# Layer norm of a two-layer vision block: the squares of three channel chunks added on GpSimd before TensorE sums them

## The chip, the cores and the metric

The kernel runs on one core of a Trainium2 chip. A core has five engines with a queue of instructions each: TensorE (PE in the profile; its weight loads are shown apart as PEld), VectorE (DVE), ScalarE (ACT), GpSimd (POOL) and SyncE (SP), which here issues most of the DMAs. The engines work on SBUF, a memory of 128 partitions; TensorE writes its results into PSUM. The metric is the device time of one execution in microseconds, as the median of several runs.

## The reference

The input x has the shape (8, 384, 64, 64), f32: eight images, 384 channels. Two layers follow each other, each with a group norm in front and a residual around it. The first is a window attention with a layer norm over the channels, the second a convolution block. Cut to what matters:

```python
def _L0_conv_ref(x, norm_g, norm_b, qkv_w, qkv_b, proj_w, proj_b, rpb1, rpb2):
    xt = x.reshape(b, c, h * w).transpose(0, 2, 1)
    mu = xt.mean(-1, keepdims=True)
    var = ((xt - mu) ** 2).mean(-1, keepdims=True)
    xt = (xt - mu) / jnp.sqrt(var + EPS) * norm_g + norm_b
    qkv = (xt @ qkv_w + qkv_b).reshape(b, h * w, 3, c).transpose(2, 0, 1, 3)
    ...
    x1 = win_attn(w1[0], w1[1], w1[2], rpb1, None)
    x2 = win_attn(w2[0], w2[1], w2[2], rpb2, ATTN_MASK2)
    ...
    out = out @ proj_w + proj_b

x = x + _L0_conv_ref(_gn(x), ...)
x = x + _L1_conv_ref(_gn(x), fft_filter, w_in, w_dw, w_out)
```

The change is in `mu` and `var`, the mean and the variance over the 384 channels of each of the 4096 pixels of an image.

## The kernel before

An image is cut into eight strips of 8 rows, 512 pixels each. A strip is a tile of 128 partitions by 3 chunks by 512 pixels (`strip`), so a pixel's 384 channels lie in 128 partitions and 3 chunks. There are 64 strips in all.

The first layer takes a strip through these pieces: `group_normal` (VectorE) writes the group-normed strip y. `ln_square` (L306) lets ScalarE write the squares of y, one instruction for all three chunks, into sq, a tile with a single buffer. `ln_sums` (L310) lets TensorE multiply y and sq with a column of 1/384, so that the sum over the partitions comes out; the three chunks are added up in PSUM, 4 groups of 128 pixels side by side in 32 columns of the array each. One matmul of the program appears as two in the trace (f32), so y and sq have 24 matmul instructions each per strip. From the sums come the variance, a square root and a reciprocal (tile lr, VectorE and ScalarE); a DMA writes the row to DRAM and another spreads it over the partitions (line, rs), and `ln_scale` (L333) multiplies y by it. `shifted_half` (L338) lets GpSimd copy halves of two strips into the strip y2 of the shifted windows (L349 to L351). Then come the attention's matmuls: pq (`qk_tile`), pvv (`v_tile`, with a memset of a column of v on GpSimd, L392), pS (`scores`), the soft maximum on VectorE and ScalarE (tile e, L429 to L439), pT (`turn`), pA (`apply`), the division by the sum (tile o, L473 and L474), po (`put`) and pr (`project`).

The second layer has pt (`mix`), pf (`transform`), pz (`back`), the border tiles z that ScalarE writes (L598 to L602), the convolution on VectorE (`conv`, L642, tile zz, one instruction per tap), the gate, pw (`finish`), and x_finish (L672), in which VectorE adds pw onto the strip and so frees the PSUM buffer. The tag gemm has four PSUM buffers; pw takes three of them at once.

All pieces are put into one plan by hand (`at(place, piece, ...)`), sorted by place and then written out, so that strips of the first layer of one image lie between strips of the second layer of the image before. TensorE's matmuls keep this order exactly (`keep_in_program_order`). The instructions of the other engines are ordered at build time by a list scheduler, which takes what is ready by its own estimate and otherwise follows the place in the program; each engine then works through its queue in order. For a strip, with v = u - 4 and u = 2s + 16b, the layer norm has these places:

```python
at(v + 0.15, group_normal, b, s)
at(v + 0.45, ln_square, b, s)
at(v + 0.99, ln_sums, b, s)
at(v + 1.35, ln_scale, b, s)
```

At the start GpSimd issues 64 small DMAs for the position bias (rpb_raw, L154), then memsets of the borders of seven z tiles (L268, L269), and copies six blocks of the packed q and k weights (`pack_qk`, L118). TensorE at the same time begins with the mean of the first image (pm, pv), the sums of strip 0, and the matmuls that prepare the weights (pb, pc, pv).

Of the kernel before, what the change touches and what calls it, by code (L numbers as in the profile page):

```python
# [9 lines left out]
ALU = mybir.AluOpType  # L10
AX = mybir.AxisListType

P = 128
KC = 3
# [18 lines left out]
def block_kernel(ctx: ExitStack, tc: tile.TileContext, out, x, consts, fsel, wqk, wv, bqk, bv,  # L33
                 wp, bp, lng, lnb, rpb1, rpb2, w_in, w_dw, w_out, filt):
    nc = tc.nc
# [8 lines left out]
    def psum(name):  # L44
        return ps.tile([P, ST], F32, tag="gemm", name=name)
# [6 lines left out]
    def matmul(*args, **kw):  # L52
        tc.keep_in_program_order(nc.tensor.matmul(*args, **kw))  # L53
# [4 lines left out]
    def strip(tag, bufs, name):  # L58
        return sb.tile([P, KC, ST], F32, tag=tag, bufs=bufs, name=name)

    def row512(tag, bufs, name):
        return sb.tile([P, ST], F32, tag=tag, bufs=bufs, name=name)
# [9 lines left out]
    for s in range(NS):  # L72
        tag, bufs = ("x", 5) if s < 5 else (("xn", 1), ("ow", 1), ("y2", 1))[s - 5]
        t = strip(tag, bufs, f"x_first{s}")
# [188 lines left out]
    xs, ys, y2s, qks, vs, os_, ots, x1s, zs = ({} for _ in range(9))  # L263
# [42 lines left out]
    def ln_square(b, s):  # L306
        sq = ys[b, s, "sq"] = strip("sq", 1, f"sq_{b}_{s}")
        nc.scalar.activation(sq, ys[b, s], AF.Square)

    def ln_sums(b, s):  # L310


        p = psum(f"ln_{b}_{s}")
        for to, t in ((0, ys[b, s]), (P, ys.pop((b, s, "sq")))):
            for k in range(KC):
                for j in range(4):
                    matmul(p[32 * j:32 * (j + 1), to:to + P], ones_c[:, 0:32], t[:, k, j * P:(j + 1) * P],
                           start=(k == 0), stop=(k == KC - 1))
        m = sb.tile([P, 2 * P], F32, tag="lc", bufs=1, name=f"m_{b}_{s}")
        nc.scalar.copy(m, p[:, 0:2 * P])  # L320
        rc = sb.tile([P, P], F32, tag="lr", bufs=2, name=f"lr_{b}_{s}")
        nc.vector.tensor_tensor(rc, m[:, 0:P], m[:, 0:P], ALU.mult)  # L322
        nc.vector.tensor_tensor(rc, m[:, P:2 * P], rc, ALU.subtract)
        nc.scalar.activation(rc, rc, AF.Sqrt, bias=eps_t)
        nc.vector.reciprocal(rc, rc)

        line = dr.tile([4, P], F32, tag="line", bufs=4, name=f"line_{b}_{s}")
        queue = nc.scalar if b == 0 and s < 2 else nc.sync
        queue.dma_start(out=line, in_=rc[0:P:32, :])
        rs = ys[b, s, "rs"] = row512("rs", 2, f"rs_{b}_{s}")  # L330
        queue.dma_start(out=rs, in_=bass.AP(line.tensor, line.offset, [[0, P], [1, ST]]))
# [347 lines left out]
    for b in range(B):  # L679
# [17 lines left out]
        for s in range(NS):  # L697
# [3 lines left out]
            at(v - 0.84, load, b, s, "norm")  # L701
# [5 lines that stand above are left out]
# [162 lines left out]
```

## Time and profile before

The profile is of one execution. Its device time was 3803.7 us, of which the span from the first to the last instruction is 3801.9 us.

| what | us |
|---|---|
| median of 3 runs | 3809.83 |
| lowest and highest run | 3804.54 and 3810.86 |
| device time of the profiled execution | 3803.7 |
| span of the profiled execution | 3801.9 |
| mean granted TensorE clock | 0.994 |
| TensorE, 24 matmuls ln<-y per strip, busy in all 64 strips | 56.3 |
| TensorE, 24 matmuls ln<-sq per strip, busy in all 64 strips | 54.3 |
| ScalarE, one square of a strip (64 of them) | 1.484 median |
| GpSimd, copy 128x384 f32, L349 (112 into y2) | 0.504 shortest, 0.506 median, 1.437 longest |
| VectorE, one tap of the convolution, L642 (1490) | 0.654 shortest, 0.747 median, 0.993 longest |
| TensorE waiting in pt for VectorE's x_finish | 14.5 in all, 11 times, longest 2.5 |

How to read it: busy is the time in which at least one instruction of the kind runs; matmuls overlap, so 24 of 0.27 us each can be busy for 0.85 us only. In a timeline a line gives the start and the length in us, the engine, the line of the kernel, the operation, the tile written and the tiles read, the shape, and how many instructions were merged; in square brackets stands how long the engine had been idle before and what ended that.

### The profile page before, as it was taken

Reading aid. Unit: us, or ns where it says so; the run is one execution under the profiler, and the core shown is the slowest. Engines: PE = TensorE matmul, PEld = TensorE weight load, DVE = VectorE, ACT = ScalarE, POOL = GpSimd, SP = SyncE. Lnnn points to the kernel's source line nnn. Section 1 sums busy time; section 2 is a strip of 40 time slices with the busy share of each in tenths; the row PEclk is TensorE's granted clock in tenths of the full one; section 3 lists DMA queues with packets and bytes.
Section 4 is the critical chain, followed back from the end, with each engine's and each line's share of the span. In section 5 each row is a group of like instructions: output and inputs, shape, how many; then the busy total and the mean of one; then the engine's idle time right before and its main releaser. Section 6 shows DMA issues by size and latency. Waiting matters only on the chain.

```text
span 3801.9 us, 90288 instructions
## 1 busy us (share of the span) xinstructions
PE 3681.0 (97%) x39168; PEld 2350.2 (62%) x39168; DVE 2822.1 (74%) x4601; ACT 2458.7 (65%) x3997; POOL 273.0 (7%) x648
## 2 busy tenths in 40 slices
PE   6999999999999999999999999999999999999998
PEld 4666666666666665666666666666666666666554
DVE  5555577768777678777878777778778777677898
ACT  3766577657667576666767666666676667676442
POOL 4000000000000000000000000000000000000000
PEclk9999999999999999999999999999999999999999
DMA  4322222223322223223322323323233222221422
GB/s 120 99 86 83 89 92 102 90 95 115 115 92 93 109 88 121 97 82 112 115 104 103 107 80 107 123 79 107 91 119 107 98 95 73 97 80 71 159 100 75
DMA packets 144496, 377.16 MB, mean 99 GB/s; under 512 B 12308, under 2 KB 12900, under 8 KB 144100
## 3 DMA queue, kind: packets, MB, share of 16 engines
q1 hardware_dynamic: 139952, 370.60, 27.5%
q8 instruction: 308, 5.05, 0.6%
q0 software_dynamic: 2048, 0.15, 0.1%
q10 hardware_dynamic: 2100, 0.63, 0.1%
q14 instruction: 88, 0.72, 0.1%
HBM read 270.54 MB, written 100.79 MB: 98 GB/s over the span
## 4 chain that ended last, share of the span: by engine, by line
PE 82%; DVE 10%; DMA 3%; ACT 2%; issue 2%; SPq 0%; DVEq 0%; ACTq 0%
PE pq L53 22%; PE pt L53 13%; PE pr L53 12%; PE pvv L53 11%; PE pw L53 6%; DVE zz L642 4%; PE pS L53 3%; PE pz L53 3%; PE pT L56 3%; PE pA L53 2%; PE ln L53 2%; PE po L56 2%; PE pf L53 2%; DMA rs<-line 1%; PE pc L53 1%
## 5 line engine op out<-in xcount | busy, mean ns | idle before, releaser
L642 DVE SCALAR_TENSOR_TENSOR zz<-z,dw_sb,zz 128x512 f32<-128x512 f32 x1490 | 1094.8, 751 | 132.5 <-ACT z L601 114.6
L53 PE MATMUL pq<-y,wqk_sb 128*128 128x512 f32 x2160 | 990.6, 596 | 0.4 <-issue 0.4
L53 PEld LDWEIGHTS pq<-y,wqk_sb 128*128 128x128 f32 x2160 | 403.1, 190 | 457.4 <-issue 426.2
L53 PE MATMUL pt<-wi_sb,xn 128*128 128x384 f32 x1536 | 540.7, 490 | 14.5 <-DVE x_finish L672 14.5
L53 PE MATMUL pr<-oT,wp_sb 128*128 128x512 f32 x1152 | 523.5, 593 | 1.1 <-DVE oT L507 1.0
L53 PE MATMUL pvv<-wv_sb,y 128*128 128x192 f32 x2880 | 495.8, 326 | 0.0
L53 PEld LDWEIGHTS pvv<-wv_sb,y 128*128 128x128 f32 x2880 | 471.7, 190 | 36.2 <-issue 21.8
L53 PEld LDWEIGHTS pt<-wi_sb,xn 128*128 128x128 f32 x1536 | 287.9, 191 | 223.8 <-issue 60.0
L367 ACT ACTIVATE qab<-pq,bq_sb,cst 96x512 f32<-96x512 f32 (+1 forms) x256 | 197.2, 770 | 303.0 <-PE pq L53 301.3
L367 ACT ACTIVATE kcd<-pq,vec 32x512 f32<-32x512 f32 x512 | 348.8, 681 | 8.9
L53 PEld LDWEIGHTS pr<-oT,wp_sb 128*128 128x128 f32 x1152 | 210.9, 190 | 225.1 <-issue 210.9
L322 DVE TENSOR_TENSOR lr<-m 128x128 f32<-128x128 f32 x64 | 18.8, 294 | 437.3 <-ACT m L320 437.3
L553 ACT COPY t<-pt 128x384 f32<-128x384 f32 x256 | 122.8, 480 | 194.4 <-PE pt L53 191.8
L401 ACT COPY v<-pvv 128x384 f32<-128x384 f32 x256 | 121.6, 479 | 177.2 <-PE pvv L53 176.9
L367 ACT ACTIVATE qcd<-pq,bq_sb,cst 96x512 f32<-96x512 f32 (+1 forms) x256 | 197.9, 773 | 56.3 <-PE pq L53 49.2
L516 DVE SCALAR_TENSOR_TENSOR x_add<-pr,vec,x_add 128x512 f32<-128x512 f32 x192 | 143.5, 748 | 120.2 <-PE pr L53 118.4
L349 POOL COPY y<-y 128x384 f32<-128x384 f32 x112 | 99.8, 891 | 1741.9 <-PE pvv L53 1243.6
L636 ACT ACTIVATE zz<-z,dw_sb 128x512 f32<-128x512 f32 x183 | 133.2, 732 | 89.0 <-PE pw L53 56.0
L367 ACT ACTIVATE kab<-pq,vec 96x512 f32<-96x512 f32 (+1 forms) x256 | 174.8, 683 | 21.5 <-PE pq L53 19.4
L439 ACT ACTIVATE e<-e 128x1024 f32<-128x1024 f32 x128 | 135.4, 1058 | 74.9 <-DVE e L434 73.8
L53 PE MATMUL pw<-zz,wo_sb 128*128 128x512 f32 x384 | 182.9, 612 | 0.0
L56 PEld LDWEIGHTS po<-cst,o 128*128 128x128 f32 x1024 | 119.7, 141 | 64.2 <-issue 62.8
(139 smaller groups left out, 5286.9 us busy)
## 6 DMA issues: line engine op xcount, KB each, us to landing
x_add<-in_x_dram SPq DMA_DIRECT2D x64, 768.0 KB, 9.6
x1d<-x_add SPq DMA_DIRECT2D x64, 768.0 KB, 3.6
x_mix<-x1d SPq DMA_DIRECT2D x64, 768.0 KB, 4.3
x_finish<-x1d SPq DMA_DIRECT2D x64, 768.0 KB, 4.4
out_dram<-x_finish SPq DMA_DIRECT2D x64, 768.0 KB, 4.5
x_norm<-in_x_dram SPq DMA_DIRECT2D x61, 768.0 KB, 7.4
x_stats<-in_x_dram SPq DMA_DIRECT2D x56, 768.0 KB, 7.5
rs<-line SPq DMA_DIRECT2D x62, 256.0 KB, 3.0
```

The costliest lines, as they stand in the source:

```text
L53: tc.keep_in_program_order(nc.tensor.matmul(*args, **kw))
L56: tc.keep_in_program_order(nc.tensor.transpose(*args, **kw))
L322: nc.vector.tensor_tensor(rc, m[:, 0:P], m[:, 0:P], ALU.mult)
L349: nc.gpsimd.tensor_copy(dst[:, :, :, :, 0:4], src[:, :, :, :, 4:8])
L367: return nc.scalar.activation(dst[to:to + n], pq[of:of + n], AF.Identity, bias=bias[of:of + n], scale=scale)
L401: nc.scalar.copy(v[:, 2 * g:2 * g + 2, :, 0:HD], pvv[:, 0:384].rearrange("p (g h d) -> p g h d", g=2, h=4))
L439: nc.scalar.activation(e, e, AF.Exp)
L516: nc.vector.scalar_tensor_tensor(t[:, m, :], pr, bp_sb[:, m:m + 1], t[:, m, :], ALU.add, ALU.add)
L553: nc.scalar.copy(t1, pt[:, 0:C])
L636: nc.scalar.activation(zz.rearrange("p (r c) -> p r c", c=SW), z[:, 1:9, 1:SW + 1], AF.Copy, scale=dw_sb[:, m, 4:5])
L642: i = nc.vector.scalar_tensor_tensor(acc.rearrange("p (r c) -> p r c", c=SW), z[:, dy:dy + 8, dx:dx + SW], dw_sb[:, m, TAPS[tap]:TAPS[tap] ...
```

## The change

After ScalarE has written the squares, GpSimd adds the second and then the third chunk of them onto the first, in place. TensorE then sums the squares of one chunk instead of three; its sums of y stay as they were. So `ln_square` gets two instructions on GpSimd for each strip, of 128 partitions by 512 pixels with two inputs in SBUF, and `ln_sums` has 4 matmuls of the program over sq (8 instructions) instead of 12 (24).

```diff
     def ln_square(b, s):
         sq = ys[b, s, "sq"] = strip("sq", 1, f"sq_{b}_{s}")
         nc.scalar.activation(sq, ys[b, s], AF.Square)
+        for k in (1, 2):
+            nc.gpsimd.tensor_tensor(sq[:, 0, :], sq[:, 0, :], sq[:, k, :], ALU.add)
 
     def ln_sums(b, s):
 
 
         p = psum(f"ln_{b}_{s}")
-        for to, t in ((0, ys[b, s]), (P, ys.pop((b, s, "sq")))):
-            for k in range(KC):
+        for to, t, n in ((0, ys[b, s], KC), (P, ys.pop((b, s, "sq")), 1)):
+            for k in range(n):
                 for j in range(4):
                     matmul(p[32 * j:32 * (j + 1), to:to + P], ones_c[:, 0:32], t[:, k, j * P:(j + 1) * P],
-                           start=(k == 0), stop=(k == KC - 1))
+                           start=(k == 0), stop=(k == n - 1))
         m = sb.tile([P, 2 * P], F32, tag="lc", bufs=1, name=f"m_{b}_{s}")
```

## The prediction

> **What bounds the kernel now.** I read the page first: busy shares, then the chain of waits.
>
> ```profile
> PE 3681.0 (97%) x39168; PEld 2350.2 (62%) x39168; DVE 2822.1 (74%) x4601; ACT 2458.7 (65%) x3997; POOL 273.0 (7%) x648
> ...
> PE 82%; DVE 10%; DMA 3%; ACT 2%; issue 2%; SPq 0%; DVEq 0%; ACTq 0%
> ```
>
> TensorE (PE) is busy 97% of 3801.9 us and is 82% of the chain: its matmuls run in the written order, and what is taken out of them comes off the end, unless another engine is then late. Next, TensorE in a strip from the middle, in order of time (start, length, line, operation).
>
> ```profile
> 1515.51 2.10 PE L53 MATMUL pt<-wi_sb,xn 128*128 128x384 f32 x6
> ...
> 1533.27 0.86 PE L53 MATMUL ln<-y,cst 128*32 128x128 f32 x24
> 1533.95 0.84 PE L53 MATMUL ln<-sq,cst 128*32 128x128 f32 x24
> 1534.72 0.88 PE L53 MATMUL pf<-t,cst 64*64 64x192 f32 x16
> ```
>
> The 24 matmuls over sq follow the 24 over y with no gap. From start to start the first 24 take 0.68 us, 0.0283 us each; those over sq take 0.77 us up to the next group. The squares for them were made by ScalarE (ACT) long before:
>
> ```profile
> 1503.47 1.49 ACT L308 ACTIVATE sq<-y 128x1536 f32<-128x1536 f32 x1 [2.68 <-DVE y L303]
> ```
>
> They end at 1504.96 and are first read at 1533.95: 29.0 us of slack. Comparing the 64 squares with the 64 sums, strip 0 has 0.05 us, strip 1 has 1.5 us, and strips 2 to 63 have 14.4 to 45.5 us. GpSimd (POOL) has nothing to do in most of this time:
>
> ```profile
> 1505.29 0.13 POOL L392 MEMSET v<- 128x16 f32 x1 [15.33 <-PE pA L53]
> 1533.48 0.50 POOL L349 COPY y<-y 128x384 f32<-128x384 f32 x1 [28.06 <-PE pvv L53]
> ...
> 1544.60 1.44 POOL L349 COPY y<-y 128x384 f32<-128x384 f32 x1 [7.80 <-DVE y L336]
> 1545.98 0.93 POOL L350 COPY y<-y 128x336 f32<-128x336 f32 x1
> ```
>
> The same copy takes 0.50 us once and 1.44 us another time. The VectorE (DVE) timeline says why:
>
> ```profile
> 1505.99 2.74 DVE L642 SCALAR_TENSOR_TENSOR zz<-z,dw_sb,zz 128x512 f32<-128x512 f32 x4 [2.56 <-ACT z L601]
> ...
> 1513.91 0.68 DVE L672 TENSOR_TENSOR x_finish<-pw,x_finish 128x512 f32<-128x512 f32 x1
> ...
> 1544.45 1.22 DVE L434 TENSOR_TENSOR e<-e,mx 128x1024 f32<-128x1024 f32 x1
> 1545.59 0.99 DVE L642 SCALAR_TENSOR_TENSOR zz<-z,dw_sb,zz 128x512 f32<-128x512 f32 x1
> ```
>
> The copy issued at 1544.60 ends 0.37 us after the VectorE instruction that had begun at 1544.45, and the next VectorE instruction takes 0.99 us where the usual one takes 0.74. They exclude each other. The last two views are of the start, TensorE and GpSimd:
>
> ```profile
> 35.61 1.51 PE L53 MATMUL ln<-sq,cst 128*32 128x128 f32 x24 [0.86 <-ACT sq L308]
> 37.05 3.15 PE L53 MATMUL pb<-vec,wqk_sb 128*128 128x1 f32 x14
> ```
>
> ```profile
> 40.01 5.79 POOL L154 DMA_DIRECT2D rpb_raw<-in_rpb_dram  x10 [0.21 <-issue]
> 45.73 0.20 POOL L268 MEMSET z<- 128x10 f32 x1
> ```
>
> Strip 0's sums run at 35.61, while GpSimd's own queue is occupied with 64 small bias loads until 45.8.
>
> **What the Trainium skill says.** "GPSIMD Engine Reference", section "3.1 Elementwise — side-by-side cycle accounting", has a two-input f32 add of 2048 elements at 4497 ns. A quarter of it is 1.12 us; with some 0.05 us of start I take 1.17 us for 128x512, an estimate. No two-input operation on GpSimd is in this trace; the nearest row, the one-input copy of 384 elements at 0.50 us undisturbed, sets a floor of about 0.65 us for 512. "SBUF — State Buffer", section "Who interferes with whom", says that a VectorE instruction with two SBUF inputs and a GpSimd instruction that reads SBUF hold the shared port exclusively, for the whole instruction. The copies above agree (0.50 to 1.44, 0.74 to 0.99).
>
> **The change, part by part.**
>
> Removed: 16 of 24 matmuls per strip, each with its weight load. At 0.0283 us each that is 0.453 us, times 62 strips 28.1 us. Strip 0 runs colder: its group takes 1.44 us (35.61 to 37.05), of which two thirds, 0.96, go; strip 1 gives 0.5. Sum: 29.5 us. The groups next to it wait on nothing that would keep them there, so I count it whole.
>
> Added, wait in the steady strips: the two adds take 2.4 us after the square, and 14.4 us or more are free before the sums. GpSimd's waiting copies (L349) come later in its order. What is queued on GpSimd behind the adds, the memset of v and the copies, has slack of its own. Cost 0. The single sq buffer is given back by the sums as before.
>
> Added at the start: strip 0's adds can't run before GpSimd's queue is through. The z memsets (L268, L269) have no input and stand behind all 64 loads; the adds come later in the program, so they stand behind those too. The memsets end near 46.3; two adds of 1.17 end near 48.7. TensorE, in order, then starts at 48.8 what it started at 35.61: 13.2 us. Behind it are pb, pc, strip 1's sums, the v weights and the first pq, with gaps under 1 us up to 60 us, so nothing absorbs it. If the six weight copies (L118, 2.1 us) go first, it is 15.3; if the adds get into the queue earlier, 0. I take 13.2. Strip 1's adds hide behind pb and pc (8.2 us).
>
> Added on VectorE: the adds start as the square ends, and in about half of the strips VectorE's convolution begins then. I put two exclusive adds of 1.17 us into the VectorE timeline of each of the 49 strips that have convolution beside them. In the strip shown the first add runs 1505.0 to 1506.2 and costs the instruction waiting at 1505.99 0.2 us; that one runs; the second add then holds up the next by 1.17. Sum 1.36 us. VectorE is without a gap from there to x_finish (1513.91, ends 1514.59), which frees the PSUM buffer of pt, started at 1515.51. With 0.05 us for the signal 0.87 us of slack is left, so TensorE stalls 0.49 us. Over the strips:
> - six where convolution starts 0.66 us after the square: delay 1.7 (one 2.4), slack 0.15, stalls 10.1 us
> - five where it is already running: delay 2.34 (one 0.74), slack 0.05, stalls 9.9 us
> - five with convolution 1.03 us after, slack to 0.16: delay 1.35, stalls 6.6 us
> - three with slack 0.6 to 0.9, the one shown among them: 2.7 us
> - thirty with more slack, or with VectorE idle at the adds: 0.2 us
>
> Together 29.5 us, by chance equal to the gain. Adds of 0.8 us give 15.8, of 1.35 give 37.7; of 0.25, what the trace shows a copy to cost, 2.5. Zero is the floor: an add gives VectorE nothing.
>
> **Sum.** -29.5 + 13.2 + 29.5 = +13.2 us on the profiled execution: span about 3815, device time about 3817 from 3803.7. That execution is 6 us below the median of the runs, 3809.83; put on the median, 3823.
>
> **Rivals.**
> - As forecast, 3823: own range 3813 to 3833.
> - Soft port (the other side, not slower): while both engines read, VectorE loses only about 0.5 us per add, not the whole add; stalls 6.7 us. -29.5 + 13.2 + 6.7 = -9.6, 3800. Its place is convolution after the square; it decides from where the stalls fall under 16.3 us, an add that holds VectorE for 0.8 us or less. For it: a copy cost 0.25 us. Against: the copies waited a whole 1.22 us instruction, so the exclusion looks whole.
> - Free start: the adds get in ahead of the loads, or the delay is absorbed. -29.5 + 29.5 = 0, 3810. Against it: the memsets' place in the queue.
> - Both, soft port and free start: -22.8, 3787.
> - Heavier: adds of 1.35 us, and the weight copies ahead (start 13.2 + 2.1 + 0.4 = 15.7): -29.5 + 15.7 + 37.7 = +23.9, 3834. A few us more come if the memset of v, which waits for pA, stands in front of the adds.
>
> **Numbers.** Chances: as forecast 0.42, heavier 0.19, soft port 0.20, free start 0.12, both 0.07. 0.2% is 7.6 us, about what a measurement can tell from no change. Faster: both 0.07, most of soft port 0.14, a little of the free start 0.02: 0.23. Same: soft port 0.06, free start 0.08, the low edge of the forecast 0.07: 0.21. Slower: 0.56. Range 3795 to 3839: below lies the better part of "both", above the tail of "heavier".
>
> **What would show it.** Eight matmuls ln<-sq per strip and about 0.3 us for them; the first ln<-sq at 48 to 51 us with GpSimd as what TensorE waited for; the wait of pt for x_finish up from 14.5 us (11 times) to some 40; convolution instructions of 1.5 to 1.9 us just after the square; GpSimd busy some 150 us more. I am wrong if sums in mid-kernel wait for GpSimd, if the first sums run near 36 us, or if the wait for x_finish hardly grows.

## The result, and the profile after

The changed kernel takes 3826.12 us (median of 4 runs, 3824.85 to 3828.28); the kernel before, beside it, 3807.18 us. The ratio is 1.0051 with a 95% interval of 1.0033 to 1.0068: slower by 19 us. A second set of runs of the same two kernels gave 1.0067 (1.0053 to 1.0080). The profiled execution spans 3826.5 us.

First the page of the changed kernel, busy shares and chain of waits:

```profile
PE 3663.0 (96%) x38144; PEld 2324.6 (61%) x38144; DVE 2867.4 (75%) x4601; ACT 2455.7 (64%) x3997; POOL 446.5 (12%) x776
...
PE 72%; DVE 19%; DMA 4%; issue 3%; ACT 2%; POOL 0%; ACTq 0%; DVEq 0%; POOLq 0%
```

TensorE has 1024 matmuls fewer and 18 us less to do, and yet the span is longer. In the chain that ended last TensorE has gone from 82% to 72%, VectorE from 10% to 19%. VectorE has the same 4601 instructions; they take 45 us more. GpSimd itself is busy 174 us more and is 0% of the chain. What costs is what it does to VectorE, and the one wait at the start.

The list of TensorE's waits (who waited for whom; total, times, longest):

```profile
PE pt L53 <- DVE x_finish L674: 25.1, 15, 3.5
PE ln L53 <- POOL sq L310: 14.5, 1, 14.5
PE pt L53 <- ACT g L655: 9.2, 6, 1.6
```

The middle line is a single wait, at the start. The first was 14.5 us in 11 waits before; the third is new. In its six strips the first x_finish and the gelu named there end within 0.1 us of each other, and both stand behind the same late convolution on VectorE, so the two lines belong together.

The start, on TensorE and then on GpSimd:

```profile
34.02 1.58 PE L53 MATMUL ln<-y,cst 128*32 128x128 f32 x24 [1.13 <-DVE y L303]
...
50.14 0.65 PE L53 MATMUL ln<-sq,cst 128*32 128x128 f32 x8 [14.54 <-POOL sq L310]
50.72 4.00 PE L53 MATMUL pb<-vec,wqk_sb 128*128 128x1 f32 x18
```

```profile
46.99 0.24 POOL L269 MEMSET z<- 128x10 f32 x1
47.13 1.38 POOL L310 TENSOR_TENSOR sq<-sq 128x512 f32<-128x512 f32 x1
48.34 0.53 POOL L118 COPY wqk_sb<-wqk_raw 128x48 f32<-128x48 f32 x2
48.72 1.36 POOL L310 TENSOR_TENSOR sq<-sq 128x512 f32<-128x512 f32 x1
```

The square of strip 0 was ready at 36.4, but its adds came after the last bias load and the last memset, and two weight copies slipped between the two adds. TensorE began pb at 50.7 instead of 37.05. A further part of the start is no wait. The second group of pb, in the change and then before:

```profile
67.92 3.84 PE L53 MATMUL pb<-vec,wqk_sb 128*128 128x1 f32 x18
```

```profile
53.35 2.06 PE L53 MATMUL pb<-vec,wqk_sb 128*128 128x1 f32 x18
```

The same 18 matmuls took 1.8 us longer. The granted TensorE clock was 0.63 from 60 to 70 us and 0.69 from 70 to 80, where the kernel before had 1.00 in both. In a second profile of the change (e9) it was 0.65 and 0.67, and pb took 3.84 us again. Why the clock was lower here no run shows. From 100 to 3500 us its mean is 1.00 in both kernels, so the rest of the loss is not a matter of the clock.

A strip in the middle, one in which the convolution begins 1.03 us after the square. VectorE, GpSimd, TensorE:

```profile
1984.18 3.86 DVE L644 SCALAR_TENSOR_TENSOR zz<-z,dw_sb,zz 128x512 f32<-128x512 f32 x4 [2.62 <-ACT z L603]
...
1993.22 0.67 DVE L674 TENSOR_TENSOR x_finish<-pw,x_finish 128x512 f32<-128x512 f32 x1
```

```profile
1983.21 2.95 POOL L310 TENSOR_TENSOR sq<-sq 128x512 f32<-128x512 f32 x2 [15.13 <-ACT sq L308]
```

```profile
1991.41 1.04 PE L56 MATMUL po<-cst,o 128*128 128x128 f32 x8
1993.95 2.20 PE L53 MATMUL pt<-wi_sb,xn 128*128 128x384 f32 x6 [1.50 <-DVE x_finish L674]
```

The four taps of the convolution take 3.86 us where they took 2.74 before. The two adds, 1.27 us each when nothing is in their way, take 2.95 together: each engine waits for the other. VectorE's next instructions follow without a gap, x_finish ends at 1993.89, and pt, which needs the PSUM buffer, stands still for 1.50 us. In the same strip before it stood for 0.25:

```profile
1970.65 2.20 PE L53 MATMUL pt<-wi_sb,xn 128*128 128x384 f32 x6 [0.25 <-DVE x_finish L672]
```

Where the time went can be counted from TensorE's timelines, since its order is the same in all these kernels. Each row is a stretch from the first instruction of one group to the first of another, summed over its occurrences, as the difference to the kernel before in us (profiled executions; e1 to e8 are the experiments below; pw stands for its last six matmuls, pw<-zz):

| stretch (occurrences) | change | e1 | e2 | e3 | e4 | e5 | e6 | e7 | e8 |
|---|---|---|---|---|---|---|---|---|---|
| start, up to 100 us | 16.8 | -0.4 | 4.8 | 2.2 | -0.1 | -0.7 | -0.8 | -0.1 | 16.0 |
| ln to the next po (62) | -30.3 | -31.2 | -30.4 | -0.9 | -29.0 | -1.8 | -1.5 | -26.3 | -3.9 |
| po to pt (53) | 22.1 | 24.5 | -1.6 | 21.8 | -1.3 | -1.1 | 3.7 | -1.6 | -1.4 |
| pt to the next pT (52) | 7.6 | 6.6 | -2.2 | 5.5 | -1.3 | -0.5 | 2.5 | -2.1 | -3.9 |
| pT to the next pw (53) | 6.0 | 8.5 | 4.1 | 2.2 | -0.4 | 7.9 | 4.3 | 6.4 | 12.3 |
| pT to the next ln (62) | 0.0 | 0.6 | 0.0 | 0.0 | 10.5 | 0.0 | 0.0 | 0.0 | 0.0 |
| all, up to the last pw | 25.0 | 12.2 | -25.6 | 33.3 | -20.5 | 2.7 | 7.3 | -23.0 | 20.7 |

The row from pT to pw is no part of what the adds do. It holds most of TensorE's stops that the trace puts down to no wait ("issue"). These stops do not fall at random: their places go with TensorE's sequence of instructions. Counting stops of over 0.3 us by strip and tile, the change has 40 and e2, which has the same sequence, 38, and 34 of them are in the same places. The kernel before and e3, again with one sequence, share 28 (of 39 and 34). The change and the kernel before share only 13. All "issue" stops together take 36.3 us before and 34.2 to 36.7 in e3, e5 and e6, which have its sequence; 41.0 in the change, 37.6 in e9, 39.0 in e2; 38.5 to 41.8 in e1, e4 and e7; 45.6 in e8. So taking matmuls out moved these stops, and in these profiles made them some us longer. What causes them no run shows.

They are in other rows too. From ln to po they take 3.8 us before, 1.5 in the change and 1.3 in e2. The median of this stretch went from 7.45 us to 7.02 in both, which is 0.44 us a strip and 27 us for 62; the rest of the 30 us in this row is in good part stops that now lie elsewhere.

The profiled execution of the kernel before was a quick one (3803.7 us; its runs beside the change took 3803.3 to 3810.9). Single profiled spans compare to some 5 us; the ratios decide.

### The profile page after: what moved, and what is told of

It reads as the page before. It is cut to its first block, busy times and chain, and to the rows that moved or that the text cites. A ratio compares the mean times of both kernels' runs of the same rounds, so it can differ in the third digit from the quotient of the medians.

```text
span 3826.5 us, 88262 instructions
## 1 busy us (share of the span) xinstructions
PE 3663.0 (96%) x38144; PEld 2324.6 (61%) x38144; DVE 2867.4 (75%) x4601; ACT 2455.7 (64%) x3997; POOL 446.5 (12%) x776
## 3 DMA queue, kind: packets, MB, share of 16 engines
q1 hardware_dynamic: 139952, 370.60, 27.3%
## 4 chain that ended last, share of the span: by engine, by line
PE 72%; DVE 19%; DMA 4%; issue 3%; ACT 2%; POOL 0%; ACTq 0%; DVEq 0%; POOLq 0%
PE pq L53 19%; PE pt L53 13%; PE pvv L53 11%; PE pr L53 10%; DVE zz L644 9%; PE pw L53 4%; PE pT L56 2%; PE pS L53 2%; PE pA L53 2%; DMA rs<-line 2%; PE pz L53 2%; PE po L56 2%; PE ln L53 2%; PE pf L53 1%; DVE st L220 1%
## 5 line engine op out<-in xcount | busy, mean ns | idle before, releaser
L644 DVE SCALAR_TENSOR_TENSOR zz<-z,dw_sb,zz 128x512 f32<-128x512 f32 x1490 | 1132.5, 776 | 131.4 <-ACT z L603 114.9
L310 POOL TENSOR_TENSOR sq<-sq 128x512 f32<-128x512 f32 x128 | 176.4, 1378 | 647.0 <-ACT sq L308 642.1
```

What stands on the lines that cost most here:

```text
L310: nc.gpsimd.tensor_tensor(sq[:, 0, :], sq[:, 0, :], sq[:, k, :], ALU.add)
L644: i = nc.vector.scalar_tensor_tensor(acc.rearrange("p (r c) -> p r c", c=SW), z[:, dy:dy + 8, dx:dx + SW], dw_sb[:, m, TAPS[tap]:TAPS[tap] ...
```

## The experiments

All ratios are against runs of the kernel before on the same chip; its medians were 3803.2 to 3806.4 us in these sets.

**e1: strips 0 and 1 of the first image as before.**

```diff
-        for k in (1, 2):
+        for k in (1, 2) if b or s > 1 else ():
...
-        for to, t, n in ((0, ys[b, s], KC), (P, ys.pop((b, s, "sq")), 1)):
+        for to, t, n in ((0, ys[b, s], KC), (P, ys.pop((b, s, "sq")), 1 if b or s > 1 else KC)):
```

> The change, but strips 0 and 1 of the first image keep their three-chunk sums on TensorE and have no adds. Theory (the loss is a wait for GpSimd's queue at the start plus VectorE held up later): the 14.5 us wait of the first ln<-sq goes and with it some 14 to 17 us of the span, so the time falls from 19 us above the kernel before to 0 to 6 us above it; the wait of pt for x_finish stays near 25 us. Rival (the start is absorbed later, the whole loss is contention): no more than 3 us are won, 15 to 19 us above before.

Measured: 3817.11 us against 3806.36, ratio 1.0033 (1.0021 to 1.0045), 10.8 us above before, between the two ranges. The wait at the start is gone; x_finish holds up pt for 28.6 us. So the start is a real part of the loss, and what remains without it is larger than was expected. In this profile 5.5 us of the rest are longer stops (41.8 against 36.3).

**e2: the saving without the adds.** The kernel leaves two of three chunks of the squares out.

```diff
         nc.scalar.activation(sq, ys[b, s], AF.Square)
-        for k in (1, 2):
-            nc.gpsimd.tensor_tensor(sq[:, 0, :], sq[:, 0, :], sq[:, k, :], ALU.add)
```

> The sums as in the change, but no adds at all: the squares of the second and third chunk are left out of the variance, for all 64 strips. Theory: TensorE's saving alone, 29 to 31 us faster than the kernel before (ratio 0.992), no wait of TensorE for GpSimd, pt waiting some 14 us for x_finish. Rival (TensorE's saving turns mostly into waits for VectorE and ScalarE anyway): 5 to 15 us faster, with the waits of pt, pz and pw grown by the rest.

Measured: 3780.96 us, ratio 0.9939 (0.9927 to 0.9952), 25.4 us faster, somewhat under the range. pt waits 13.0 us for x_finish, and the waits of pz and pw for VectorE and ScalarE are as before within 0.5 us. So the saving does not turn into waits for these engines. What is missing is not settled: in this one execution 4.8 us lie in the start and 2.7 in longer stops.

**e3: the adds without the saving.** e1 with TensorE summing three chunks in every strip.

```diff
-(P, ys.pop((b, s, "sq")), 1 if b or s > 1 else KC)):
+(P, ys.pop((b, s, "sq")), KC)):
```

> The adds on GpSimd for all strips but 0 and 1 of the first image, while TensorE still sums all three chunks: the first chunk then holds the sum already, so the variance counts two chunks twice. The adds' cost without their gain. Theory (adds hold VectorE out of its second SBUF input, and x_finish comes late): 25 to 34 us slower than the kernel before, some 30 more in the stretch from po to pT of the strips with convolution. Rival (soft port, the loss is elsewhere): 0 to 10 us slower.

Measured: 3843.21 us, ratio 1.0097 (1.0083 to 1.0111), 36.9 us slower: the theory's direction, above the top of its range. The profile shows it where it was expected, 27.3 us from po to pT. TensorE's sequence is that of the kernel before, so this is the cleanest measure of what the adds cost. e2 and e3 together make 1.0036; e1, which has both, is 1.0033. The parts add up within the intervals.

**e4: the adds later.** A piece of its own, after VectorE's x_finish; strips 0 and 1 as in e1.

```diff
+    def ln_add(b, s):
+        sq = ys[b, s, "sq"]
+        for k in (1, 2):
+            i = nc.gpsimd.tensor_tensor(sq[:, 0, :], sq[:, 0, :], sq[:, k, :], ALU.add)
+            if k == 1:
+                tc.add_manual_dep(i.ins, zs["gate"].ins.name, ...)
...
+            if b or s > 1:
+                at(v + 0.75, ln_add, b, s)
```

> The change with strips 0 and 1 of the first image as before, and the adds of a strip waiting for ScalarE's move of the second branch's first q tile, which comes after VectorE's x_finish, some 13 us later than in the change and 12 to 16 us before the sums need them. Theory: the adds then hold up VectorE where nothing on TensorE waits for it within 3 us; pt waits for x_finish 10 to 16 us as before, and the time is 22 to 30 us below the kernel before. Rival (the adds cost the same wherever they stand, because VectorE is short of time in every stretch): 0 to 10 us above before. A third: the sums of some strips wait for GpSimd, and the gain is below 15 us.

Measured: 3789.01 us, ratio 0.9956 (0.9944 to 0.9969), 17.4 us faster; the place decides, though less is won than the theory said. x_finish is back at 13.5 us. What is missing is in a line that was not there before (TensorE's waits of e4):

```profile
PE pvv L53 <- ACT kcd L375: 6.8, 6, 1.1
```

In six strips the adds now meet other two-input work of VectorE. One of them, VectorE and ScalarE:

```profile
1341.32 1.66 DVE L663 TENSOR_TENSOR g<-g,zz 64x512 f32<-64x512 f32 x1
```

```profile
1345.81 0.35 ACT L513 COPY oT<-po 128x224 f32<-128x224 f32 x1 [2.02 <-DVE oT L515]
```

The same instruction on g took 0.69 us before. VectorE comes to its part of oT later, ScalarE, which follows it there, waits 2.02 us where it waited 0.97, its moves are done later, and pvv waits: 10.5 us from pT to ln in the table, 1.4 us in each of six strips and less in others. The adds took 1.60 us in the median here, so they were still being shut out by VectorE.

**e5: GpSimd writes, but does not read.** e3 with memsets in place of the adds.

```diff
+            nc.gpsimd.memset(sq[:, 0:2, :], 1.0)
```

> In place of the two adds, two memsets on GpSimd of 128x1024 each, which write SBUF and read nothing; TensorE sums three chunks; strips 0 and 1 of the first image without them. The first two chunks of the squares are thereby overwritten with ones. Theory (it is GpSimd's reading that shuts out VectorE's second SBUF input): within 4 us of the kernel before, pt waiting 12 to 17 us for x_finish, the four taps after the square 2.74 us as before. Rival (any GpSimd work on SBUF at this moment holds VectorE up): as much as the adds for the same busy time, 20 us or more slower.

Measured: 3808.08 us against 3805.75, ratio 1.0004 (0.9996 to 1.0012). GpSimd and VectorE in a strip of e5:

```profile
1503.86 1.96 POOL L310 MEMSET sq<- 128x1024 f32 x2 [15.10 <-ACT sq L308]
```

```profile
1504.84 2.74 DVE L644 SCALAR_TENSOR_TENSOR zz<-z,dw_sb,zz 128x512 f32<-128x512 f32 x4 [2.62 <-ACT z L603]
```

GpSimd writes until 1505.82, a microsecond into the convolution, and the four taps take 2.74 us as before. GpSimd work that only writes does not hold VectorE up, so the rival is out. That reading is what excludes fits the adds and the one-input copies that the prediction shows.

**e6: one-input copies in place of the adds.**

```diff
+            nc.gpsimd.tensor_copy(sq[:, 0, :], sq[:, k, :])
```

> In place of the two adds, two one-input copies of 128x512 on GpSimd, into the first chunk; TensorE sums three chunks; strips 0 and 1 of the first image without them. The first chunk of the squares is thereby replaced by the third. Theory (VectorE is shut out for as long as the GpSimd instruction reads): a copy takes some 0.63 us, half of an add, and the slack before pt takes its part off first, so 7 to 15 us slower than before, less than half of what the adds alone cost (36.9). Rival (the cost goes by the number of instructions, not by their length): 30 us or more.

Measured: 3811.10 us against 3805.75, ratio 1.0017 (1.0011 to 1.0024), about 6.5 us slower (4 to 9 by the interval), at the low edge of the range. GpSimd and VectorE in a strip of e6:

```profile
1505.04 1.29 POOL L310 COPY sq<-sq 128x512 f32<-128x512 f32 x2 [15.10 <-ACT sq L308]
```

```profile
1506.01 2.84 DVE L644 SCALAR_TENSOR_TENSOR zz<-z,dw_sb,zz 128x512 f32<-128x512 f32 x4 [2.62 <-ACT z L603]
```

The two copies are through 0.3 us after the convolution begins and cost it 0.1 us. That rules out a price per instruction as high as with the adds. That VectorE is held for the whole of GpSimd's instruction it doesn't show, because the copies mostly miss the convolution; another instruction does, in the last section.

**e7: the adds later still**, gated by the move of the third q tile instead of the first.

```diff
             if t == 0:
-                zs["gate"] = i
+            zs["gate" if t == 0 else "late"] = i
...
-                tc.add_manual_dep(i.ins, zs["gate"].ins.name, ...)
+                tc.add_manual_dep(i.ins, zs["late"].ins.name, ...)
```

> As the version with the adds later, but they wait for ScalarE's move of the third q tile of the second branch instead of the first, some 8 us later again, where VectorE has least to do, and still some 4 us before the sums. Theory: the six stalls of pvv of 1.1 to 1.4 us that the earlier place had go away, and the time is 20 to 28 us below the kernel before. Rival: the sums of some strips now wait for GpSimd (a wait of ln for sq of more than 5 us in all), and it is not faster than the earlier place.

Measured: 3780.83 us against 3805.75, ratio 0.9931 (0.9919 to 0.9944): 24.9 us faster than the kernel before and some 45 faster than the change. GpSimd, and below VectorE at the same moment:

```profile
1516.73 2.61 POOL L313 TENSOR_TENSOR sq<-sq 128x512 f32<-128x512 f32 x2 [20.45 <-ACT qcd L375]
```

```profile
1515.40 1.88 DVE L220 BATCH_NORM_STATS2 st<-x_stats 128x6 f32<-128x512 f32 x3 [1.08 <-DMA x_stats<-in_x_dram]
1517.32 0.81 DVE L227 BATCH_NORM_AGGREGATE mv_a<-st 128x2 f32<-128x144 f32 x1
1523.96 0.29 DVE L330 TENSOR_TENSOR lr<-m 128x128 f32<-128x128 f32 x1 [5.84 <-ACT m L328]
```

VectorE has one-input work there and then 5.8 us of nothing, the adds run at their own length (1.27 us in the median), and TensorE's waits for them come to 1.1 us in all (six weight loads). The interval covers e2, the version without any adds (0.9939): at this place they cost nothing that can be measured (to some 5 us).

**e8: the start alone.**

```diff
-        for k in (1, 2):
+        for k in () if b or s > 1 else (1, 2):
...
-(P, ys.pop((b, s, "sq")), 1)):
+(P, ys.pop((b, s, "sq")), KC if b or s > 1 else 1)):
```

> The adds and the one-chunk sums for strips 0 and 1 of the first image alone; the other 62 strips as before. Theory (the first sums wait for GpSimd's queue, and nothing absorbs it): the first ln<-sq at 48 to 51 us after a wait of 13 to 15, and 12 to 15 us slower than the kernel before. Rival (absorbed later in the first image, where engines other than TensorE set the pace for a while): the wait is there, and the time is 0 to 7 us above before.

Measured: 3821.28 us, ratio 1.0035 (1.0023 to 1.0047): 13 us slower by the ratio, 15.5 by the medians, from a change to two strips of 64. The rival, 0 to 7 us, is out. In e8's list of TensorE's waits:

```profile
PE ln L53 <- POOL sq L310: 14.4, 1, 14.4
```

Followed along TensorE's order, e8 is 16.0 us behind at the place that the kernel before reaches at 94 us, 15.5 us at the one of 437 us and 16.9 at the one of 563. So the first image wins nothing back. Later the distance goes between 12 and 23 us, where the stops (45.6 us against 36.3) have moved and the rows ln to po and pt to pT are 3.9 us shorter each: the total is not the start alone.

**e9: the change again.**

> The change itself, unaltered, beside a new set of runs of the kernel before. The start alone was 1.0035 and the rest alone (strips 0 and 1 as before) 1.0033. If the two parts add up, and nothing absorbs one of them: 1.0068, 24 to 28 us above before. If a part of the start is won back when the steady strips are changed as well: 1.004 to 1.0055, 15 to 21 us.

Measured: 3827.70 us against 3803.22, ratio 1.0067 (1.0053 to 1.0080). e8 and e1 make 1.0035 and 1.0033, together 1.0068, so this set speaks for parts that add up. The first set of the change, 1.0051, lies in the range of the rival (1.004 to 1.0055). The two intervals overlap between 1.0053 and 1.0068; that some us are won back after the first image is not excluded.

## Why the prediction was right, and where its terms were off

The forecast was 3823 in a range of 3795 to 3839, for the reasons that the runs then showed. Term by term:

- **TensorE's saving, -28.1 us for 62 strips.** Right: the median stretch behind ln is 0.44 us shorter, where 0.453 were forecast. The 30.3 us of the table are more only because "issue" stops moved out of this stretch. That the stops would move and grow was not in the forecast.
- **The start, +13.2, less 1.5 saved in strips 0 and 1.** The place and the cause were right, the first sums ran at 50.14 in the forecast window of 48 to 51. In the profiles the term was too small: 16.8 us in the change, 16.0 in e8, where 11.7 were forecast; the runs of e8 (13 to 15.5, with an interval of 9 to 18) don't decide this. The adds took 1.37 us each instead of 1.17, two weight copies came between them, that execution's statistics were 0.85 us late, TensorE waited 1.64 us for wv_sb where it had waited 0.87, and pb ran 1.8 us longer at the lower clock. The first image wins nothing back, as forecast (e8).
- **VectorE held up, +29.5.** The mechanism was right: the waits and the longer convolution came where they were forecast. From pw over po and pt to pT, TensorE loses 31.1 us in the change (22.1, 7.6 and 1.4 from pw to po); the runs of e3 lose 36.9. One mis-sized part is the add: 1.27 us measured, 1.17 estimated from a quarter of the figure in the Trainium skill ("GPSIMD Engine Reference", section "3.1 Elementwise — side-by-side cycle accounting"). Between the forecast's own two points (29.5 for 1.17, 37.7 for 1.35) 1.27 us gives about 34. That the sum came so near is partly luck, since by groups of strips the errors cancel. The six strips with convolution 0.66 us after the square were to lose 10.1 us and lost 9.7. The five where it is already running were to lose 9.9 and lost 14.4. The five with convolution 1.03 us after and slack to 0.16 were to lose 6.6 and lost 0.8. All others were to lose 2.9 and lost 6.2. In three of the five that lost little, pw came 1.0 to 2.2 us later in the change; it did so in e2 too, which has no adds (1.1 to 2.3), and not in e3 (0.0). There the moved stops gave VectorE the time. Why the five strips with convolution already running lost more is open.
- **No wait of the steady strips for GpSimd: right.** ln waits for sq once in 64 strips.
- **The rivals.** The soft port is out: four taps lost 1.12 us where about 1.35 were forecast, sh (last section) waits until the add's end, and e3 costs more than the forecast, not less. The free start is out by e8. Of the heavier case about half came true: the longer add, and part of the weight copies.

The ratios of e2, e3 and e8 make 1.0071 together, +27 us (-23, +37, +13, each to some 5 us). The two sets of runs of the change gave +19 and +24.5, the forecast was +13.2. So 3826 against 3823 looks closer than it was: the forecast was put on a median of 3809.83 for the kernel before, and beside the change this was 3807.18. The direction did not hang on luck, but the forecast had its gain and the hold-up of VectorE equal, so that the start alone decided. In fact the hold-up exceeds the gain by itself: e3 lost 36.9 us (32 to 42 by its interval), e2 won 25.4 (18 to 28), and e1, which has both, is at 1.0033.

## What to carry to other kernels

Work moved to an idle engine was free here only where it took nothing that a busy one used: ask which two-input VectorE instructions run at the moment when GpSimd will read SBUF, and what on the bounding engine hangs on them. The adds ran as soon as their input was ready, 0.08 us after the square in the steady strips. There they cost 37 us; placed some 22 us after the square, within the 29 us of slack, they cost nothing that can be measured. And look at the first use apart from the steady state: two strips of 64 made about half of the loss, because an engine that is idle later was the one that loads at the start.

## What the runs showed of the hardware that was not expected

A tiny VectorE instruction is held up until GpSimd's ends. The shift of the second group norm (sh) has two inputs of 128x1 in SBUF and took 0.16 us before. In the change:

```profile
1352.11 1.07 DVE L537 SCALAR_TENSOR_TENSOR sh<-gs_b 128x1 f32<-128x1 f32 x1
```

The add beside it runs from 1351.88 to 1353.16, and sh ends at 1353.17. In five of its eight executions sh meets an add like this, and takes 1.05 to 1.07 us each time. In e5 it meets a memset in the same five, and takes 0.16. GpSimd's memset of 128x1024, 0.95 us of writing, also left VectorE's two-input taps at 2.74 us for four, while the adds cost them 1.12 us. This agrees with "SBUF — State Buffer" in the Trainium skill, section "Who interferes with whom", which has the exclusion between VectorE's second input and a GpSimd instruction that reads, and none with one that only writes. The prediction took from that section that the lock lasts for the whole instruction. The section calls the lock exclusive, and has the words for the whole instruction in its line on VectorE's 2-port modes; sh shows that they hold for two inputs too.
